# First expert products with weights stationary: two weight matrices fetched per tile from DRAM

## The chip, the core and the metric

The kernel runs on one NeuronCore of a Trainium2 chip. Its engines work side by side: PE (TensorE, matrix products), ACT (ScalarE), DVE (VectorE), POOL (GpSimd) and SP (SyncE, which here only issues DMAs). The metric is the device time of one execution in microseconds; of several runs the median is taken.

## The reference, cut to what matters

The input is 2048 tokens of 256 numbers (4 batches of 512). A mixture-of-experts block, an attention block and the same expert block again are added to it. All is float32.

```python
x = x + 0.5 * _L0_ffn_ref(_layernorm(x, axis=-1), gate, w0, w1, wo)
x = x + _L0_attn_ref(_layernorm(x, axis=-1), wq_a, q_a_norm_w, wq_b, wkv_a, kv_a_norm_w, wkv_b, wo_attn)
x = x + 0.5 * _L0_ffn_ref(_layernorm(x, axis=-1), gate, w0, w1, wo)

def _L0_ffn_ref(x, gate_kernel, w0_kernel, w1_kernel, wo_kernel):   # 8 experts, 256 -> 512 -> 256
    gate_logits = jnp.einsum('bsd,de->bse', x, gate_kernel)
    top_k_weights, top_k_indices = jax.lax.top_k(gate_logits, 2)
    top_k_weights = jax.nn.softmax(top_k_weights, axis=-1)
    combine = ...                      # the two weights at the two experts' places, else 0
    h0 = jnp.einsum('bsd,edm->bsem', x, w0_kernel)
    h1 = jnp.einsum('bsd,edm->bsem', x, w1_kernel)
    inter = jax.nn.silu(h0) * h1
    return jnp.einsum('bse,bsem,emd->bsd', combine, inter, wo_kernel)
```

## The kernel before, in words

Only the two chosen experts of a token are computed. The kernel sorts the (token, expert) pairs into tiles: up to 128 tokens that share one expert. Each of the two expert phases has 39 tiles (`NTILES`). A list of tiles (`list_tiles`) holds per tile the token rows (`idx`), the tokens' weights (`w`) and the offset `off` of the expert's columns in the stored weights, as an integer that an engine reads into a register. Each phase has two lists, made at different times, because the first tiles start before all tokens are routed.

The weights of all experts lie in SBUF for the whole kernel: `w_sb[0]`, `w_sb[1]` and `w_sb[2]` (w0, w1, wo), 4 MB each. `load_expert_weights` (L127) fetches them at the start on SP's queue, in loads of 1 MB.

`ffn_tiles` (L907) is a generator with one tile `j` per round:

- `gather(j + 2)` (L916): an indirect DMA of POOL fetches the token rows of the tile two rounds ahead.
- `hidden(j)` (L938): PE reads `off` (L940) and makes h0 and h1 (L951), with the turned tokens `xT` stationary (a weight of 128x128) and 512 weight columns moving, in two halves of the 256 inputs. The result has tokens as its 128 partitions. ACT takes the silu (L961), DVE the product `it` (L963).
- `turn(j + 1)` (L928): PE transposes the next tile's rows (L933), DVE copies them (L936).
- `project(j - 1)` (L974): four products with `wo` (L978) give `py`. They need the hidden numbers on the partitions, so `turn_hidden` (L966) had transposed `it` on PE (L969) and copied it on ACT (L971). DVE scales by the tokens' weights (L987) and POOL adds the rows into a DRAM tensor `acc_d` by an indirect DMA (L992); the last tiles of the second phase add into the output itself.
- `turn_hidden(it)` of tile j.

After each of the four parts the generator yields, and other work is put in there: in the first phase the routing of the later tokens and the first steps of attention, in the second the routing of the last batch (`beside.step`). Each engine executes its instructions in the order in which this program emits them; there is no scheduler after that. The same holds for SP, whose queue carries all plain loads and stores: the start's loads, a copy of x into `acc_d[0]` (L1283), the attention weights (`load_attention`), the reload of x from `acc_d[0]` (L109), the read of the routing table (L495), the stores of x into `acc_d[1]` (L1255), and the four copies of `acc_d[1]` to the output (L1004), issued when tile `final - 1` of the second phase has been projected.

A matrix product in float32 appears in the profile as two PE records, each with a weight load (PEld) of its own; a transposition as one.

Of the kernel before, what the change touches and what calls it, by code (L numbers as in the profile page):

```python
# [9 lines left out]
F32 = mybir.dt.float32  # L10
I32 = mybir.dt.int32
AF = mybir.ActivationFunctionType
# [4 lines left out]
P = 128  # L17
# [15 lines left out]
def kernel(  # L33
# [29 lines left out]
    WE = DC * MLP  # L63
# [6 lines left out]
    NTILES = (2 * NTOK + (P - 1) * NE) // P  # L70
# [15 lines left out]
    pp = ctx.enter_context(tc.tile_pool(name="p", bufs=2 * NT + LEAD))  # L86
# [3 lines left out]
    ps_a = ctx.enter_context(tc.tile_pool(name="ps_a", bufs=3, space=PSUM))  # L90
    ps_t = ctx.enter_context(tc.tile_pool(name="ps_t", bufs=2, space=PSUM))
# [30 lines left out]
    nc.scalar.dma_start(gate_sb[:, :, :NE], gate_k.rearrange("(c p) e -> p c e", p=P))  # L122


    w_sb = [wpool.tile([P, NE * WE], F32, name=f"w{i}_sb") for i in range(3)]

    def load_expert_weights(i):  # L127
        rows_of = (w0_k, w1_k, wo_k)[i].rearrange("e k m -> (e k) m")
        width = rows_of.shape[1]
        n = P * (2 * WE // width)  # L130
        for r in range(0, rows_of.shape[0], n):
            c0 = r // P * width
            nc.sync.dma_start(
                w_sb[i][:, c0 : c0 + 2 * WE].rearrange("p (k m) -> p k m", m=width),
                rows_of[r : r + n, :].rearrange("(k p) m -> p k m", p=P),
            )


    ident = const.tile([P, P], F32, name="ident")
# [510 lines left out]
    def put(pt, oh, first, last):  # L650
# [6 lines left out]
        )  # L657

    def route_first(ph, loads):


# [137 lines left out]
    def list_tiles(ph, n, m, split=0, read=None):  # L799
# [9 lines left out]
        last = m == B  # L809
        res = {"rows": NTOK + P if last else m * S}  # L810
# [4 lines left out]
        def parts():  # L815
# [91 lines left out]
    def ffn_tiles(f, jobs, final=None):  # L907

        n = len(jobs)
        xg, xT = {}, {}

        def gather(j):  # L916
            if j >= n:
                return
            res, i = jobs[j]
            xg[j] = ptp.tile([P, D], F32, tag="pt", name="xg")  # L920
            nc.gpsimd.indirect_dma_start(  # L921
                out=xg[j],
                out_offset=None,
                in_=xn_d[f][: res["rows"], :],
                in_offset=bass.IndirectOffsetOnAxis(ap=res["idx"][:, i : i + 1], axis=0),
            )

        def turn(j):  # L928
            if j >= n:
                return  # L930
            pt = ps_t.tile([P, DC, P], F32, tag="t", name="pt_x")
            for c in range(DC):
                nc.tensor.transpose(pt[:, c, :], xg[j][:, c * P : (c + 1) * P], ident)  # L933
            del xg[j]
            xT[j] = ptp.tile([P, DC, P], F32, tag="pt", name="xT")
            nc.vector.tensor_copy(xT[j], pt)  # L936

        def hidden(j):  # L938
            res, i = jobs[j]
            off = nc.values_load(  # L940
                res["off"][:, i : i + 1],
                engines=(mybir.EngineType.PE,),
                min_val=0,
                max_val=(NE - 1) * WE,
                skip_runtime_bounds_check_because="the offset of one of NE experts, or 0",
            )
            ph = []
            for w in range(2):
                p = ps_a.tile([P, MLP], F32, tag="a", name=f"h{w}")
                for c in range(DC):  # L950
                    nc.tensor.matmul(  # L951
                        p,
                        lhsT=xT[j][:, c, :],
                        rhs=w_sb[w][:, bass.ds(off + c * MLP, MLP)],
                        start=(c == 0),
                        stop=(c == DC - 1),
                    )
                ph.append(p)
            del xT[j]
            g = pp.tile([P, MLP], F32, tag="p", name="g")  # L960
            nc.scalar.activation(g, ph[0], AF.Silu)  # L961
            it = pp.tile([P, MLP], F32, tag="p", name="it")
            nc.vector.tensor_mul(it, g, ph[1])  # L963
            return off, it

        def turn_hidden(it):  # L966
            pt = ps_t.tile([P, MC, P], F32, tag="t", name="pt_i")
            for m in range(MC):
                nc.tensor.transpose(pt[:, m, :], it[:, m * P : (m + 1) * P], ident)  # L969
# [4 lines left out]
        def project(j, off, iT):  # L974
            res, i = jobs[j]
            py = ps_p.tile([P, D], F32, tag="p", name="py")
            for m in range(MC):
                nc.tensor.matmul(  # L978
                    py,
                    lhsT=iT[:, m, :],  # L980
                    rhs=w_sb[2][:, bass.ds(off + m * D, D)],
                    start=(m == 0),
                    stop=(m == MC - 1),
                )
            direct = final is not None and j >= final
            y = ptp.tile([P, D], F32, tag="pt", name="yo")
            nc.vector.tensor_scalar_mul(y, py, res["w"][:, i : i + 1])  # L987
            dst = flat_out if direct else acc_d[f][: res["rows"], :]
            held.append((dst, res["idx"][:, i : i + 1], y))
            if not direct or j >= final + HELD:  # L990
                for dst, idx, y in held:
                    nc.gpsimd.indirect_dma_start(  # L992
                        out=dst,
                        out_offset=bass.IndirectOffsetOnAxis(ap=idx, axis=0),
                        in_=y,
                        in_offset=None,
                        compute_op=ALU.add,
                    )
                held.clear()
            if final is not None and j == final - 1:  # L1000

                for r in range(0, NTOK, NTOK // 4):
                    r = slice(r, r + NTOK // 4)
                    nc.sync.dma_start(  # L1004
                        flat_out[r, :].rearrange("(p r) d -> p (r d)", p=P),
                        acc_d[f][r, :].rearrange("(p r) d -> p (r d)", p=P),
                    )

        held = []
        gather(0)  # L1010
        gather(1)
        yield -1
        turn(0)
        yield -1
        todo = None
        for j in range(n):
            gather(j + 2)
            off, it = hidden(j)
# [250 lines left out]

    list_a = route_first(one, loads)  # L1270

# [2 lines left out]
    jobs = [(list_a, i) for i in range(n_a)]  # L1274
# [46 lines left out]
    jobs = [(list_a, i) for i in range(n_a)]  # L1321
# [7 lines left out]
    for i, (b, h) in enumerate(items):  # L1329
# [13 lines left out]
        for kc in range(NT):  # L1343
# [3 lines left out]
            k = (i + 1) * NT + LEAD + kc  # L1347
# [114 lines left out]
```

## Time and profile before

| | |
|---|---|
| median of 3 runs | 1198.45 us (1195.29 to 1198.54) |
| the profiled execution's own time | 1194.49 us |
| its span | 1192.3 us |
| PE, DVE, ACT, POOL busy | 1115.8, 612.7, 452.3, 577.7 us |
| first products of the tiles (L951) | 624 records, 283.0 us |
| transpositions of the hidden numbers (L969) | 312 records, 47.9 us |
| products with wo (L978) | 624 records, 147.8 us |

The span is the time from the first to the last instruction of the profiled execution. In the rows of slices each digit is the busy share, in tenths, of one fortieth of the span. In the timeline a row gives start and duration in microseconds, the engine, the line of the kernel, the operation, what it writes and reads, and in brackets how long the engine had been idle before it and what ended that wait. PE rows of one line are merged; the duration of a merged row includes the tail of the last record, which overlaps with the next row.

### The profile page before, as it was taken

The numbers are of one execution on the slowest core, as the hardware profiler recorded it, in microseconds if no ns is written. First come the engines' busy times: TensorE is split into PE (matmuls) and PEld (weight loads), VectorE is DVE, ScalarE is ACT, GpSimd is POOL, SyncE is SP. The second block draws the span as 40 slices with busy tenths as digits, with TensorE's granted clock in tenths as the row PEclk, the third lists the DMA queues.
The fourth block names the chain that finished last, engine by engine and source line by source line (L and its number), as shares of the span: only waits on it lengthen the run. The fifth ranks groups of instructions, "written<-read, shape, count | busy, mean of one in ns | idle before, by whom it ended". The sixth has DMA issues, their size and how long they took to land. (4 is left out here: it accounts for less than half of the span.)

```text
span 1192.3 us, 15062 instructions
## 1 busy us (share of the span) xinstructions
PE 1115.8 (94%) x4704; PEld 631.8 (53%) x4704; DVE 612.7 (51%) x1673; ACT 452.3 (38%) x992; POOL 577.7 (48%) x645
## 2 busy tenths in 40 slices
PE   4889999999899999999999989899999899999995
PEld 3555666566445455444445545454455456666563
DVE  6463222344567666686666676657756343222221
ACT  4421221122554555554454544455454231121111
POOL 4244444355545454543566444475474246444342
PEclk8999999999999999998999989999999999999998
DMA  9943222322100000100000100001000124222422
GB/s 319 384 100 41 45 45 45 80 36 40 14 1 1 1 1 1 54 1 1 1 1 19 36 1 1 1 1 36 1 1 6 36 54 50 45 45 45 111 49 27
DMA packets 42141, 52.80 MB, mean 44 GB/s; under 512 B 10736, under 2 KB 34416, under 8 KB 41968
## 3 DMA queue, kind: packets, MB, share of 16 engines
q0 software_dynamic: 17184, 23.39, 11.8%
q1 hardware_dynamic: 24608, 28.45, 7.4%
q8 instruction: 40, 0.66, 0.2%
q14 instruction: 37, 0.30, 0.1%
q10 hardware_dynamic: 272, 0.01, 0.0%
HBM read 34.48 MB, written 21.54 MB: 47 GB/s over the span
## 5 line engine op out<-in xcount | busy, mean ns | idle before, releaser
L1160 POOL TENSOR_SCALAR pr<-pr,sm 128x512 f32<-128x512 f32 x256 | 177.8, 697 | 287.4 <-DVE sm L1159 242.3
L1155 ACT ACTIVATE pr<-ps,nm 128x512 f32<-128x512 f32 x256 | 176.5, 690 | 307.4 <-DVE nm L1152 281.2
L951 PE MATMUL h<-w_sb,xT 128*128 x624 | 283.0, 596 | 1.7 <-DVE xT L936 1.7
L1144 PE MATMUL ps<-k,q 128*128 128x512 f32 x512 | 274.9, 620 | 4.5 <-ACT pr L1155 4.5
L1152 DVE TENSOR_REDUCE nm<-ps 128x1 f32<-128x512 f32 x256 | 174.8, 683 | 102.6 <-PE ps L1144 101.4
L1166 PEld LDWEIGHTS pt<-ident,pr 128*128 128x128 f32 x1024 | 127.7, 142 | 157.4 <-issue 100.0
L992 POOL DMA_INDIRECT acc_d<-yo,idx x64 | 102.1, 1595 | 192.2 <-DVE yo L987 137.2
L963 DVE TENSOR_TENSOR it<-g,h 128x512 f32<-128x512 f32 x78 | 53.6, 687 | 248.0 <-PE h L951 237.5
L951 PEld LDWEIGHTS h<-w_sb,xT 128*128 128x128 f32 x624 | 113.3, 192 | 116.0 <-issue 112.7
L1166 PE MATMUL pt<-ident,pr 128*128 128x128 f32 x1024 | 156.6, 276 | 16.1 <-ACT pT L1173 13.9
L978 PE MATMUL py<-w_sb,iT 128*128 x624 | 147.8, 380 | 3.0 <-ACT iT L971 3.0
L971 ACT COPY iT<-pt_i 128x512 f32<-128x512 f32 x78 | 45.8, 587 | 269.3 <-PE pt_i L969 254.7
L1179 PE MATMUL po<-pT,low 128*64 128x512 f32 x512 | 123.8, 605 | 0.0
L978 PEld LDWEIGHTS py<-w_sb,iT 128*128 128x128 f32 x624 | 112.6, 190 | 17.1 <-ACT iT L971 4.1
L1144 PEld LDWEIGHTS ps<-k,q 128*128 128x128 f32 x512 | 80.2, 192 | 77.3 <-ACT pr L1155 36.9
L1159 DVE RECIPROCAL sm<-sm 128x1 f32<-128x1 f32 x256 | 41.3, 161 | 102.4 <-ACT pr L1155 101.9
L921 POOL DMA_INDIRECT xg<-xn_d,idx x78 | 77.8, 997 | 31.0 <-issue 18.8
L1171 DVE COPY pT<-pt 128x512 f32<-128x512 f32 x128 | 87.1, 680 | 2.2 <-PE pt L1166 2.2
L961 ACT ACTIVATE g<-h 128x512 f32<-128x512 f32 x78 | 46.6, 597 | 88.9 <-PE h L951 86.6
L1173 ACT COPY pT<-pt 128x512 f32<-128x512 f32 x128 | 73.9, 577 | 2.3 <-PE pt L1166 2.3
L987 DVE TENSOR_SCALAR yo<-py,wt 128x256 f32<-128x256 f32 x78 | 37.6, 482 | 57.9 <-PE py L978 57.9
L1193 PE MATMUL pwo<-wvo,oT 128*128 128x256 f32 x256 | 65.4, 398 | 1.8 <-ACT oT L1241 1.7
(220 smaller groups left out, 1122.0 us busy)
## 6 DMA issues: line engine op xcount, KB each, us to landing
w_sb<-in_L_ffn_w_kernel_dram SPq DMA_DIRECT2D x8, 1024.0 KB, 12.6
w_sb<-in_L_ffn_wo_kernel_dram SPq DMA_DIRECT2D x4, 1024.0 KB
x<-_attn_hidden_states_dram SPq DMA_DIRECT2D x4, 512.0 KB
xn_d<-xn POOLq DMA_DIRECT2D x8, 256.0 KB
x<-acc_d SPq DMA_DIRECT2D x4, 512.0 KB
acc_d<-x SPq DMA_DIRECT2D x4, 512.0 KB
xn_d<-xn SPq DMA_DIRECT2D x8, 256.0 KB, 3.7
out_dram<-acc_d SPq DMA_DIRECT2D x4, 512.0 KB, 7.3
```

The costliest lines, as they stand in the source:

```text
L921: nc.gpsimd.indirect_dma_start(out=xg[j], out_offset=None, in_=xn_d[f][: res["rows"], :], in_offset=bass.IndirectOffsetOnAxis(ap=res["idx" ...
L951: nc.tensor.matmul(p, lhsT=xT[j][:, c, :], rhs=w_sb[w][:, bass.ds(off + c * MLP, MLP)], start=(c == 0), stop=(c == DC - 1),)
L978: nc.tensor.matmul(py, lhsT=iT[:, m, :], rhs=w_sb[2][:, bass.ds(off + m * D, D)], start=(m == 0), stop=(m == MC - 1),)
L992: nc.gpsimd.indirect_dma_start(out=dst, out_offset=bass.IndirectOffsetOnAxis(ap=idx, axis=0), in_=y, in_offset=None, compute_op=ALU.add,)
L1144: nc.tensor.matmul(ps, lhsT=qT[:, t * P : (t + 1) * P], rhs=st[b]["k"][h % 2], start=True, stop=True,)
L1152: nc.vector.tensor_reduce(nm, ps, AX.X, ALU.max, negate=True)
L1155: nc.scalar.activation(pr, ps, AF.Exp, bias=nm, accum_out=sm)
L1160: nc.gpsimd.tensor_scalar(pr, pr, sm, 1.0, ALU.mult, ALU.mult)
L1166: nc.tensor.transpose(pt[:, t * P : (t + 1) * P], probs[t][:, kc * P : (kc + 1) * P], ident)
L1171: nc.vector.tensor_copy(s, pt)
L1173: nc.scalar.copy(s, pt)
L1179: nc.tensor.matmul(po[j * RANK : (j + 1) * RANK], lhsT=st[b]["low"][:, kc, 1, :], rhs=pts[j], start=(kc == 0), stop=(kc == NT - 1),)
```

## The change

w0 and w1 no longer lie in SBUF. `gather` reads the tile's first row `row` (256 times the expert's number, made by DVE for each list from the same product as `off`) into a register of SP, and loads this expert's w0 and w1, 512 KB each, from DRAM into one of three buffers. `hidden` makes h0 and h1 with 128x128 pieces of these weights stationary and the 128 tokens moving, so that the hidden numbers come out on the partitions; `turn_hidden` is dropped. `off` is read by PE in `project`, and `wo` alone is loaded at the start.

```diff
+    ws = ctx.enter_context(tc.tile_pool(name="ws", bufs=3))
...
-    w_sb = [wpool.tile([P, NE * WE], F32, name=f"w{i}_sb") for i in range(3)]
-
-    def load_expert_weights(i):
...
+    wo_sb = wpool.tile([P, NE * WE], F32, name="wo_sb")
+
+    def load_expert_outputs():
...
+            res["row"] = rt.tile([1, NTILES], I32, tag=f"row{last}", name="row")
+            nc.vector.tensor_scalar_mul(res["row"][:, :n], px[:1, 2, :n], D / WE)
...
         def gather(j):
             if j >= n:
                 return
             res, i = jobs[j]
+            row = nc.values_load(
+                res["row"][:, i : i + 1],
+                engines=(mybir.EngineType.SP,),
...
+            )
+            w01[j] = ws.tile([P, 2, DC, MLP], F32, tag="ws", name="w01")
+            for w, src in enumerate((w0_k, w1_k)):
+                nc.sync.dma_start(
+                    w01[j][:, w],
+                    src.rearrange("e k m -> (e k) m")[bass.ds(row, D), :].rearrange(
+                        "(c p) m -> p c m", p=P
+                    ),
+                )
...
         def hidden(j):
+
+            ph = []
+            for w in range(2):
+                p = ps_a.tile([P, MC, P], F32, tag="a", name=f"h{w}")
+                for m in range(MC):
+                    for c in range(DC):
+                        nc.tensor.matmul(
+                            p[:, m, :],
+                            lhsT=w01[j][:, w, c, m * P : (m + 1) * P],
+                            rhs=xT[j][:, c, :],
+                            start=(c == 0),
+                            stop=(c == DC - 1),
+                        )
+                ph.append(p)
+            del xT[j], w01[j]
+            g = pp.tile([P, MC, P], F32, tag="p", name="g")
+            nc.scalar.activation(g, ph[0], AF.Silu)
+            it = pp.tile([P, MC, P], F32, tag="p", name="it")
+            nc.vector.tensor_mul(it, g, ph[1])
+            return it
+
+        def project(j, it):
             res, i = jobs[j]
             off = nc.values_load(
...
-            ph = []
-            for w in range(2):
-                p = ps_a.tile([P, MLP], F32, tag="a", name=f"h{w}")
-                for c in range(DC):
-                    nc.tensor.matmul(
-                        p,
-                        lhsT=xT[j][:, c, :],
-                        rhs=w_sb[w][:, bass.ds(off + c * MLP, MLP)],
...
-        def turn_hidden(it):
-            pt = ps_t.tile([P, MC, P], F32, tag="t", name="pt_i")
-            for m in range(MC):
-                nc.tensor.transpose(pt[:, m, :], it[:, m * P : (m + 1) * P], ident)
-            iT = pp.tile([P, MC, P], F32, tag="p", name="iT")
-            nc.scalar.copy(iT, pt)
-            return iT
...
                 nc.tensor.matmul(
                     py,
-                    lhsT=iT[:, m, :],
-                    rhs=w_sb[2][:, bass.ds(off + m * D, D)],
+                    lhsT=it[:, m, :],
+                    rhs=wo_sb[:, bass.ds(off + m * D, D)],
...
-            todo = (j, off, turn_hidden(it))
+            todo = (j, it)
...
     folded = load_folded()
-    load_expert_weights(0)
...
-        for i in (1, 2):
-            load_expert_weights(i)
+        load_expert_outputs()
```

More of the change, by code (lines that the diff above doesn't have):

```diff
@@ L122 @@
     nc.scalar.dma_start(gate_sb[:, :, :NE], gate_k.rearrange("(c p) e -> p c e", p=P))
-    w_sb = [wpool.tile([P, NE * WE], F32, name=f"w{i}_sb") for i in range(3)]
-    def load_expert_weights(i):
-        rows_of = (w0_k, w1_k, wo_k)[i].rearrange("e k m -> (e k) m")
-        width = rows_of.shape[1]
-        n = P * (2 * WE // width)
+    wo_sb = wpool.tile([P, NE * WE], F32, name="wo_sb")
+    def load_expert_outputs():
+        rows_of = wo_k.rearrange("e k m -> (e k) m")
+        n = P * (2 * WE // D)
         for r in range(0, rows_of.shape[0], n):
-            c0 = r // P * width
+            c0 = r // P * D
             nc.sync.dma_start(
-                w_sb[i][:, c0 : c0 + 2 * WE].rearrange("p (k m) -> p k m", m=width),
+                wo_sb[:, c0 : c0 + 2 * WE].rearrange("p (k m) -> p k m", m=D),
                 rows_of[r : r + n, :].rearrange("(k p) m -> p k m", p=P),
@@ L913, in ffn_tiles @@
         n = len(jobs)
-        xg, xT = {}, {}
+        xg, xT, w01 = {}, {}, {}
         def gather(j):
@@ L919, in gather @@
             res, i = jobs[j]
+            row = nc.values_load(
+                res["row"][:, i : i + 1],
+                engines=(mybir.EngineType.SP,),
+                min_val=0,
+                max_val=(NE - 1) * D,
+                skip_runtime_bounds_check_because="the first row of one of NE experts, or 0",
+            )
[7 more added lines that the diff above has]
+                )
             xg[j] = ptp.tile([P, D], F32, tag="pt", name="xg")
@@ L946, in hidden @@
             )
-            ph = []
-            for w in range(2):
-                p = ps_a.tile([P, MLP], F32, tag="a", name=f"h{w}")
-                for c in range(DC):
-                    nc.tensor.matmul(
-                        p,
-                        lhsT=xT[j][:, c, :],
-                        rhs=w_sb[w][:, bass.ds(off + c * MLP, MLP)],
[L955 to L964, printed above, removed]
-        def turn_hidden(it):
-            pt = ps_t.tile([P, MC, P], F32, tag="t", name="pt_i")
-            for m in range(MC):
-                nc.tensor.transpose(pt[:, m, :], it[:, m * P : (m + 1) * P], ident)
-            iT = pp.tile([P, MC, P], F32, tag="p", name="iT")
-            nc.scalar.copy(iT, pt)
-            return iT
-        def project(j, off, iT):
-            res, i = jobs[j]
             py = ps_p.tile([P, D], F32, tag="p", name="py")
@@ L1017, in ffn_tiles @@
             gather(j + 2)
-            off, it = hidden(j)
+            it = hidden(j)
             yield j
```

## The prediction

> **What bounds the kernel now.** I read the page's head first, then the expert stages in order of time, then the shapes on the PE, then the queues. All numbers come from the profiled execution: span 1192.3 us, time 1194.49 us, which is 0.3% under the median of the runs shown (1198.45). The sum below is made against the span; the 2.2 us around it stay.
>
> ```profile
> span 1192.3 us, 15062 instructions
> PE 1115.8 (94%) x4704; PEld 631.8 (53%) x4704; DVE 612.7 (51%) x1673; ACT 452.3 (38%) x992; POOL 577.7 (48%) x645
> PE   4889999999899999999999989899999899999995
> DMA  9943222322100000100000100001000124222422
> ```
>
> The PE is near full everywhere but in the first slices; DMA is full only in the first two. The two expert stages (about 46 to 303 us and 943 to 1181 us) hold 78 tiles: L951 has 624 records, 8 to a tile. The table by stretches shows the PE busy 90.0 of 90 us between 120 and 210, and 85.0 of 85 between 1020 and 1105, so there a tile costs what its PE work costs. From 46 to 110 us it is busy 55.3 of 64.
>
> One tile in the timeline (start, duration, engine, line):
>
> ```profile
> 152.01 0.38 PE L933 MATMUL pt_x<-ident,xg 128*128 128x128 f32 x2
> 152.23 1.89 PE L978 MATMUL py<-w_sb,iT 128*128 x8
> 153.96 0.60 PE L969 MATMUL pt_i<-ident,it 128*128 128x128 f32 x4
> 154.40 3.60 PE L951 MATMUL h<-w_sb,xT 128*128 x8
> ```
>
> Read starts, not durations, since the pipeline's tail overlaps. The next pt_x starts at 157.84. So h takes 3.44 us (0.430 a record of 512 columns), pt_x 0.22, py 1.73, pt_i 0.44: 5.83 us a tile, with no gap.
>
> The shape that the change asks for, 128 columns against a freshly loaded 128x128 f32 weight, is already in the program, at L1074:
>
> ```profile
> 257.08 1.95 PE L1074 MATMUL pj<-wqc,xnT 128*128 128x128 f32 x16
> 258.87 0.60 PE L969 MATMUL pt_i<-ident,it 128*128 128x128 f32 x4
> ```
>
> Sixteen records take 258.87 - 257.08 = 1.79 us: 0.112 each. A quarter of a 512-column record would be 0.1075, so the extra weight loads nearly hide.
>
> **The change part by part.**
>
> *Products.* Per tile 8 records of 0.430 (3.44 us) become 32 of 0.112 (3.58 us): +0.14 us. Bounds for one record: 0.1075 (a quarter of L951's) and 0.117 (L1074's load busy time, 7.5 us over 64, if loads pace a longer stream). They give 0.00 and +0.30. I take 0.112, the same shape at full clock. A rule speaks against the change: the Trainium skill, page "TensorE: Matmul & The Clock Gate", section "Back-to-back issue gap", puts a sustained stream at about 81 ns for 128 columns and 131 ns for 512. Four narrow ones would then cost 2.5 times a wide one, h would take 8.5 us, and 78 tiles would lose about 395 us. Here the ratio is 4 x 0.112/0.430 = 1.04, in f32 and in this program, so the sum uses the trace.
>
> *Transposition.* Four L969 records go: -0.44 us of PE per tile. The ACT copy iT (L971, 587 ns) goes too, off the path since ACT is under half busy. Two exceptions. At the hand-over to attention the last py (309.53) waits 2.31 us for that copy; I count 1.5 us of it, since the scores behind it have waits of their own. At the very end I count no extra gain: the last scatter follows the one before by 4.44 us (1178.68 to 1183.12), its landing, however early py comes.
>
> *Registers.* On the PE four of eight register operations a tile go (42 to 51 ns, L951) and the register load (L940, 301 ns) moves behind the products. No gap shows at either place now, 3.4 us of matmuls being queued; 0. On DVE one small row product per list comes in (L900's like takes 0.15 us), four times; the first stands ahead of the first loads, 0.15 us.
>
> Over 78 tiles: (0.14 - 0.44) x 78 = -23.4 us. Where the PE waits anyway (46 to 110 us, some ten tiles, and the second stage's first few) I give back 2.0.
>
> *DMA.* Per tile SP issues one register load and two loads of 512 KB. Three buffers let tile j+3 start when the products of j end, about 13 us before they are needed. Price of one MB:
>
> ```profile
> DMA packets 7918, 13.28 MB, mean 379 GB/s; under 512 B 512, under 2 KB 3340, under 8 KB 7916
> ...
> q1 hardware_dynamic: 7261, 11.29, 91.2%
> ```
>
> This is the stretch from 10 to 45 us: 1.05 MB at 379 GB/s is 2.8 us, half of a 5.5 us tile. Gather and scatter use 27% now (120 to 210 us), so about 0.77 in all. The skill's page "DMA: Bandwidth & Descriptors", section "Measured (HBM→SBUF, 128 partitions, SWDGE, issued from GpSimd)", gives 6.15 us for 1 MB and advises batches of at least that size. At 6.15 us per tile the queue would be the bound, +0.33 us over today's 5.82, some +25 us. The loads here run two tiles ahead back to back on SP's queue, so the trace's rate counts and the latency is covered; 0 in the steady part.
>
> *SP's order.* Loads now stand in line with SP's other work, and three places cost.
>
> First start. The row is known when off is, at 39.5 us. Two tiles' loads (2 MB) are issued then; the queue is free, since 8 MB of early loads are gone (today SP issues expert weights until 48). They land about 45 to 47; h starts at 46.6 today. About 0. But tile 2's load stands behind the 2 MB copy into acc_d and all attention loads, which take SP from 51.6 to 66.2 us today. Starting near 44, SP is free near 59, and tile 2's weights land near 63.5. Its products start at 62.28 today and about a microsecond earlier without pt_i: +2 (bounds 0 and 4).
>
> The reload of x from acc_d near 211 us waits for a scatter, and tile loads are queued behind it. They have over two tiles to spare. It also shares the queue, and POOL's next scatter waits for it; today this already costs one PE wait of 1.09 us at 228.93. +1 (0 to 2).
>
> The copies to the output:
>
> ```profile
> 1101.63 1.59 POOL L992 DMA_INDIRECT acc_d<-yo,idx  x1 [2.93 <-DVE yo L987]
> 1105.25 2.45 SPq L1004 DMA_DIRECT2D out_dram<-acc_d  x4
> 1112.74 3.60 PE L951 MATMUL h<-w_sb,xT 128*128 x8
> 1115.54 1.62 POOL L992 DMA_INDIRECT out_dram<-yo,idx  x1 [8.50 <-DMA out_dram<-acc_d]
> ```
>
> SP waits for the scatter, issues four copies until 1107.7, and only then loads the weights of the tile whose products are shown at 1112.74. Those bytes follow 2 MB of copies in the same queue (traffic ends at 1113), so the first half lands near 1116. The new timetable wants it near 1111.7. PE stall 4 us. In return today's PE wait of 1.42 us at 1129.40, for a gather behind the backlog of scatters, should vanish. +2.6 (0 to 6).
>
> **Sum.** -23.4 - 1.5 + 2.0 + 0.15 + 2 + 1 + 2.6 = -17 us. Span about 1175, its time about 1177; carried to the median (+4), 1181 us.
>
> **The rivals.**
>
> *The gain in full:* SP's three places stay covered. -23.4 - 1.5 + 2 = -23, about 1175 by the median; 1170 if a record costs 0.110. For it: each place has only a few microseconds' shortfall. Against: the copies' place is short by arithmetic.
>
> *Loads pace the long stream at 0.117:* +0.30 - 0.44 = -0.14 a tile, -11 us, given back by SP's places and the early tiles: about 1194, near no change. For it: 32 loads in a row are longer than any in this trace. Against: L1074's load starts are 0.11 apart all through.
>
> *Slower: the scatter chain on POOL becomes the bound.* Each scatter into acc_d waits for the landing of the one before. Where there is a backlog the rows stand at their minimum:
>
> ```profile
> 1124.65 1.57 POOL L992 DMA_INDIRECT out_dram<-yo,idx  x1 [2.99 <-DVE yo L987]
> 1129.11 1.58 POOL L992 DMA_INDIRECT out_dram<-yo,idx  x1 [1.57 <-DVE it L963]
> 1133.54 1.57 POOL L992 DMA_INDIRECT out_dram<-yo,idx  x1 [1.53 <-DMA out_dram<-yo,idx]
> ```
>
> 4.45 us apart, with almost no other traffic. Behind them on POOL stands the next gather, and for it the PE. A saturated queue stretches such transfers: the first gather took from 39.63 to 45.60, a late one from 1126.52 to 1129.40, so up to +3.1 us. The chain decides from 5.53 us on, and the kernel gets slower when stretching exceeds about 1.4 us. At +1.6 us (half of the bound) the tile is 6.05, +0.23 x 78 = 18 us over today, minus the hand-over's gain and plus SP's places about 1220. Against it: weights move from about 1.5 us after h ends for 2.8 us, while the scatter's bytes start about 2.4 us into the next h; by these times they overlap some half microsecond, so the chain would be near 5 us.
>
> That the change doesn't do what it says is not a case here: the instruction order has 16 products of 128x128 to a tile, each issued as two records, and no L969.
>
> **How the numbers follow.** Forecast (about -17) 0.55; gain in full 0.12; loads pace 0.13, split 0.04 faster, 0.06 the same, 0.03 slower; scatter chain 0.20, of which 0.02 only eats the gain up. About 0.3% is what a measurement of this kernel tells from no change. Faster 0.71, same 0.08, slower 0.21. The range runs from the full gain with the cheapest record, 1170, to the lower half of the scatter case, 1207; the forecast's own range is 1174 to 1188.
>
> **What would show it.** Right: between 120 and 210 us and 1020 to 1105 the PE stays full; starts of h are 5.5 us apart, 3.6 us from h to pt_x; pt_i is gone; one PE wait for a weight load after the copies, of about 4 us, and a small one at tile 2. Wrong: h over 3.8 us (loads), waits of pt_x for xg tile after tile with scatters over 5.5 us apart (chain), or waits for weight loads in the steady part (DMA).

## The result, and the profile after

The kernel got slower: 1213.24 us by the median of 4 runs (1209.25 to 1215.49) against 1196.87 us of the kernel before (4 runs beside it), a ratio of 1.0136 with a 95% interval of 1.0100 to 1.0172. The forecast was 1181 us. The profiled execution of after took 1213.32 us, its span 1211.3, which is 19.0 us over the span before; its mean granted clock was 0.969 (before 0.982).

The head of the page, and of its slices of the span the PE, its clock and the DMA:

```profile
span 1211.3 us, 18471 instructions
PE 1107.8 (91%) x6264; PEld 775.0 (64%) x6264; DVE 612.3 (51%) x1677; ACT 406.0 (34%) x914; POOL 577.5 (48%) x645
...
PE   4888999799999999999899989999999997999795
...
PEclk8989999899999999998999989999999998999898
DMA  9776888665100000100000100000002587887762
```

The PE is busy for 8 us less than before, and yet the span is longer. In both expert stages the digits of the DMA row, mostly 2 and 3 before, are now 5 to 8, and the PE row has three 7s where it had none.

One tile in the timeline (columns as in the timeline of before; L963 is now the first products, L951 pt_x, L989 py):

```profile
151.77 3.73 PE L963 MATMUL h<-xT,w 128*128 128x128 f32 x32
155.34 0.38 PE L951 MATMUL pt_x<-ident,xg 128*128 128x128 f32 x2
155.56 1.89 PE L989 MATMUL py<-wo_sb,it 128*128 x8
157.29 0.94 PE L963 MATMUL h<-xT,w 128*128 128x128 f32 x7
```

From h to pt_x it is 3.57 us for 32 records, 0.112 each; from one h to the next 5.52 us. The forecast tile was 5.83 - 0.30 = 5.53 us. What else the stretches show is in the table by stretches (busy time of PE, PEld, DVE, ACT and POOL with their instructions, granted clock, DMA share, GB/s):

```profile
120.00:210.00 90.00, 90.00 (x690) 86.70 (x689) 24.08 (x48) 10.15 (x17) 42.68 (x34) 1.00 0.87 241
210.00:303.00 93.00, 84.26 (x600) 76.06 (x599) 35.62 (x93) 12.13 (x21) 42.18 (x34) 0.96 0.65 185
...
1105.00:1181.00 76.00, 67.99 (x489) 63.53 (x488) 17.41 (x34) 7.07 (x12) 28.39 (x22) 0.96 0.72 228
```

The last two of these stretches before:

```profile
210.00:303.00 93.00, 91.86 (x357) 56.20 (x356) 37.63 (x96) 20.87 (x36) 46.29 (x37) 1.00 0.27 50
...
1105.00:1181.00 76.00, 73.89 (x282) 46.04 (x280) 19.12 (x38) 14.81 (x25) 30.32 (x23) 1.00 0.33 68
```

Between 120 and 210 us nothing is lost although the DMA engines are 0.87 busy. In the two stretches that have other traffic of their own the PE is idle for 8.7 and 8.0 us (before, 1.1 and 2.1), and its clock is lower.

The start of each tile's first products, set against before, gives the ledger. In an even stretch it falls by 0.305 us a tile; every jump above that is a loss. The fourth column is the same jump in the first experiment below (the products alone), in which no tile loads weights:

| place | forecast | loss measured | of it without loads | who waits in after |
|---|---|---|---|---|
| tile 2 | +2 | +3.5 | 0.4 | PE 2.47 us at 62.02, for its weights |
| tiles 5 to 8, a list of tiles is read | part of the 2.0 given back | +5.2 | 3.5 | PE 0.97 at 103.46 for xg, 3.90 at 106.92 for the list |
| tile 28, after the reload of x | +1 | +7.1 | 2.0 | PE 6.07 at 227.31 for xg |
| tile 33 | none | +2.3 | 0.2 | PE 2.12 at 270.20 for xT |
| tiles 47 to 51, routing of the last batch | none | +11.3 | 0.0 | PE 1.73, 3.47 and 2.71 from 995 to 1020 |
| tile 67, after the copies to the output | +2.6 with the next row | +5.5 | 0.0 | PE 5.32 at 1122.20, for its weights |
| tiles 68 to 77 | in the row above | +7.2 | 3.9 | PE five short waits for xg |
| hand-over to attention | -1.5 | -1.5 | -2.6 | |

The seven losses sum to 42 us, against a gain of 0.305 x 78 = 24; 10 of the 42 come without any load. The rest up to the 19.0 us of the span are the hand-over, the first tiles of the second stage, where the PE waits anyway and nothing is won (1.5), and small differences at other tiles. For the wait at tile 2 the profile names an operation of DVE (L373) that is no input of the products. Their xT was ready at 61.42, and SP issued their weights only at 58.93, so it is read here as a wait for the weights; in the variant below that asks for them a tile earlier it is gone.

The PE's waits, by what it waited for (total, times, longest):

```profile
PE pt_x L951 <- DMA xg<-xn_d,idx: 12.4, 8, 6.1
...
PE h L963 <- DMA w<-in_L_ffn_w_kernel_dram: 5.3, 1, 5.3
```

Before, pt_x's waits for gathers were 3.3 us in all. And POOL's waits, with two rows that before did not have among its longest ten:

```profile
POOL acc_d L1003 <- DMA acc_d<-yo,idx: 18.4, 5, 5.2
POOL out_dram L1003 <- DMA out_dram<-yo,idx: 15.4, 5, 4.4
```

These are scatters that wait for the landing of the scatter before, and behind each stands the next gather. The copies to the output, the place shown of before, read now:

```profile
1115.71 2.46 SPq L1015 DMA_DIRECT2D out_dram<-acc_d  x4
1118.76 26.61 SPq L932 DMA_DIRECT2D w<-in_L_ffn_w_kernel_dram  x12
1127.52 5.84 PE L963 MATMUL h<-xT,w 128*128 128x128 f32 x32 [5.32 <-DMA w<-in_L_ffn_w_kernel_dram]
```

The weights issued at 1118.76 behind the copies' 2 MB are there at 1127.5. Then the products run at a lower clock: 5.68 us to the next pt_x at 1133.20 instead of 3.57. The granted clock stands at 0.50 in five such stretches of the two stages in which it was 1.00 before, each behind one of the waits (3.90, 6.07, 1.73, 2.71 and 5.32 us). It does not follow every wait: after the one of 3.47 us it stayed at 1.00. Of a table of the five, the last row and the sum:

```profile
1127.50:1131.70 4.20, 4.18 (x19) 4.20 (x20) 0.00 (x0) 0.39 (x1) 0.38 (x1) 0.50 1.07 385
sum 18.20, PE 18.17 PEld 16.34 DVE 3.37 ACT 0.39 POOL 3.39; mean PE 3.63 PEld 3.27 DVE 0.67 ACT 0.08 POOL 0.68
```

The 19 records of that row take 0.22 us each, twice the 0.112 of the even stretch. So by an estimate half of the 18.2 us, some 9 of the 42, is the lower clock; the rest is mostly the waits themselves. The scatters behind the copies:

```profile
1126.26 1.62 POOL L1003 DMA_INDIRECT out_dram<-yo,idx  x1 [8.88 <-DMA out_dram<-acc_d]
1133.98 1.59 POOL L1003 DMA_INDIRECT out_dram<-yo,idx  x1 [6.11 <-issue]
1139.80 1.57 POOL L1003 DMA_INDIRECT out_dram<-yo,idx  x1 [4.23 <-DVE it L975]
...
1145.20 1.58 POOL L1003 DMA_INDIRECT out_dram<-yo,idx  x1 [2.52 <-DVE it L975]
```

They follow each other after 7.7, 5.8 and 5.4 us. Before, the backlog at this place had 4.45 us from one to the next, and so caught up with the tiles; now it does not.

### The profile page after: what moved, and what is told of

Read it like the earlier page. It is cut to its first block, busy times and chain, and to the rows that moved or that the text cites. A ratio compares the mean times of both kernels' runs of the same rounds, so it can differ in the third digit from the quotient of the medians.

```text
span 1211.3 us, 18471 instructions
## 1 busy us (share of the span) xinstructions
PE 1107.8 (91%) x6264; PEld 775.0 (64%) x6264; DVE 612.3 (51%) x1677; ACT 406.0 (34%) x914; POOL 577.5 (48%) x645
## 5 line engine op out<-in xcount | busy, mean ns | idle before, releaser
L963 PE MATMUL h<-xT,w 128*128 128x128 f32 x2496 | 300.9, 280 | 14.1 <-DVE xT L954 5.7
L963 PEld LDWEIGHTS h<-xT,w 128*128 128x128 f32 x2496 | 297.7, 197 | 21.6 <-DVE xT L954 8.0
L1155 PE MATMUL ps<-k,q 128*128 128x512 f32 x512 | 271.9, 614 | 4.5 <-ACT pr L1166 4.5
L989 PE MATMUL py<-wo_sb,it 128*128 x624 | 152.7, 389 | 0.8 <-PE pt_x L951 0.2
L989 PEld LDWEIGHTS py<-wo_sb,it 128*128 128x128 f32 x624 | 115.1, 194 | 17.9 <-issue 4.4
L1190 PEld LDWEIGHTS po<-pT,low 128*64 128x64 f32 x512 | 31.6, 138 | 49.0 <-issue 49.0
```

Source lines behind the costliest of these rows:

```text
L963: nc.tensor.matmul(p[:, m, :], lhsT=w01[j][:, w, c, m * P : (m + 1) * P], rhs=xT[j][:, c, :], start=(c == 0), stop=(c == DC - 1),)
L989: nc.tensor.matmul(py, lhsT=it[:, m, :], rhs=wo_sb[:, bass.ds(off + m * D, D)], start=(m == 0), stop=(m == MC - 1),)
L1155: nc.tensor.matmul(ps, lhsT=qT[:, t * P : (t + 1) * P], rhs=st[b]["k"][h % 2], start=True, stop=True,)
L1190: nc.tensor.matmul(po[j * RANK : (j + 1) * RANK], lhsT=st[b]["low"][:, kc, 1, :], rhs=pts[j], start=(kc == 0), stop=(kc == NT - 1),)
```

## The experiments

Ratios are to the kernel before, run beside each group of kernels on one chip (its medians there were 1194.42, 1197.31 and 1200.73 us). Three theories stood at the start. *Traffic:* 1 MB a tile on the shared DMA engines delays what POOL's gathers and scatters move. *Order:* the loads stand in SP's line behind other work and come late. *Products:* narrow products cost more than the even stretch shows.

### Which half of the change costs

**The products alone.** The kernel before with the new products: all weights at the start, as before, no transposition; each tile uses expert 0's w0 and w1. The products, set against those of the change:

```diff
-                        lhsT=w01[j][:, w, c, m * P : (m + 1) * P],
+                        lhsT=w_sb[w][:, c * MLP + m * P : c * MLP + (m + 1) * P],
```

> The kernel before with the new products and without the transposition; all weights are loaded at the start as before the change, and every tile uses the first expert's (values not the reference's). Unlike the run without loads (1194 us, whose first tile's gather waited for a copy into acc_d that SP now issued 10 us earlier), SP's start is that of before. Theory: the products do save 0.3 us a tile and the start took it back there: 1180 to 1186, h of the first tile at about 46 us. If it is near 1194 again, the saving is lost somewhere else and not by the start.

Measured: 1184.31 us (4 runs), ratio 0.9887 (0.9832 to 0.9941). So the products and the dropped transposition are worth 13 us by themselves. In its profile 0.305 us a tile are won through both stages, and some is given back with no load in sight. The PE waits 4.8 us for the list at tile 7 (before 1.7), 2.2 us for a gather after the reload of x (before 1.09), and 3.5 us for a gather behind the backlog of scatters after the copies (before 1.42):

```profile
107.85 0.38 PE L876 MATMUL px<-sel,tab 128*128 128x30 f32 x2 [4.78 <-DVE tab L510]
226.49 0.44 PE L933 MATMUL pt_x<-ident,xg 128*128 128x128 f32 x2 [2.22 <-DMA xg<-xn_d,idx]
1118.32 0.53 PE L933 MATMUL pt_x<-ident,xg 128*128 128x128 f32 x2 [3.54 <-DMA xg<-xn_d,idx]
```

Faster tiles only come to these places earlier. The whole 24 us were not to be had.

**The loads alone.** The change's loads under the products of before, with moving weights and the transposition:

```diff
+                        lhsT=xT[j][:, c, :],
+                        rhs=w01[j][:, w, c, :],
...
+            todo = (j, turn_hidden(it))
```

> The other half of the change alone: products with tokens stationary and the transposition as before the change, but w0 and w1 fetched per tile as in the change. If the loads are the loss, they cost here about what they cost in the changed kernel, some 43 us less what a longer tile (5.82 instead of 5.52 us) leaves as slack: 1225 to 1240 us. If the narrow products are the loss, it stays near 1197.

Measured: 1227.06 us (4 runs), 1.0257 (1.0189 to 1.0326), 31 us slower. The two halves add up: -1.1% and +2.6% make +1.5%, and the change has +1.4%. *Products* is out. The profile is of an execution of 1218.35 us, below this median. In it the jumps lie at the same places (tile 28 +4.0, tiles 47 to 50 +9.6, 67 to 77 +8.0), and between them a tile starts exactly 5.82 us after the other: 3.02 us behind before at tiles 7 to 27, 16.06 at tiles 50 to 66.

**Half the bytes.** w0 of expert 0 stays in SBUF for all tiles, w1 is loaded per tile.

```diff
-            for w, src in enumerate((w0_k, w1_k)):
+            for w, src in enumerate((w1_k,)):
...
-                            lhsT=w01[j][:, w, c, m * P : (m + 1) * P],
+                            lhsT=(w01[j][:, 0] if w else w0_sb)[:, c, m * P : (m + 1) * P],
```

> The changed kernel with half the bytes: w0 of the first expert is loaded once and used for all tiles (values not the reference's), w1 is fetched per tile, with the same register load and the same waits on SP. Theory traffic (the weights' bytes stretch POOL's gathers and scatters on the shared DMA engines): waits of PE for xg fall to well under half, scatters in a backlog stand about 5 us apart instead of 6, total 1180 to 1190. Theory order (the loads stand too late in SP's queue): the order is the same, so the PE waits for weights at tile 2 (2.5 us) and after the output copies (5.3 us) stay to within a microsecond or two.

Measured: 1191.16 us (20 runs), 0.9967 (0.9945 to 0.9990). Beside the products alone (0.9887) half the bytes cost 0.8%, all of them 2.5%; and yet a load of each tile stands in SP's line as in the change. The wait for weights after the copies is still 3.9 us.

**No loads per tile; expert 0's weights loaded once at the start,** and none of the others.

```diff
+    def load_first_expert():
+        for w, src in enumerate((w0_k, w1_k)):
+            nc.sync.dma_start(w01_sb[:, w], src[0].rearrange("(c p) m -> p c m", p=P))
...
-                            lhsT=w01[j][:, w, c, m * P : (m + 1) * P],
+                            lhsT=w01_sb[:, w, c, m * P : (m + 1) * P],
```

> The changed kernel without the loads per tile: w0 and w1 of the first expert are loaded once and used for all tiles, so the values are not the reference's; products, order and everything else as changed. If the loss comes with the loads (their bytes on the DMA engines, or their place in SP's queue), it vanishes here and the PE's own saving stays: about 1197 - 24 = 1173 us, starts of h 5.5 us apart in the even stretches, no PE wait over 1.5 us for xg. If narrow products themselves are the cost, it stays near 1213.

Measured: 1194.08 us (20 runs), 0.9989 (0.9964 to 1.0014), far from what was expected. The reason is mostly at the start. Before, SP is held by the loads of all experts' weights and issues the 2 MB copy of x into acc_d at 51.55. Freed of them it issues it at 41.53, beside the first gathers: pt_x waits 4.79 us for xg, the first products start 5.9 us late and run at a lower clock (h 6.5 us), and at tile 1 it is 8.1. The products alone, above, keep the start's loads and do not show this. So this kernel does not measure what it was meant to. But it shows a start that is 8 us later when 2 MB move beside the first gathers.

### Order or traffic

**Weights three tiles ahead, in four buffers.** The loads of tile 2 are out ahead of the acc_d copy, and each load has a tile more of time. Gathers are two ahead, as in the change.

```diff
-    ws = ctx.enter_context(tc.tile_pool(name="ws", bufs=3))
+    ws = ctx.enter_context(tc.tile_pool(name="ws", bufs=4))
...
-            gather(j + 2)
+            ahead("w", j + 3, fetch)
+            ahead("x", j + 2, gather)
```

> The changed kernel with four weight buffers instead of three and the weights asked for three tiles ahead, gathers still two. Theory order: both PE waits for weights vanish and with them about 9 us: 1204 or less. Theory traffic: the waits for weights vanish too, but the waits of pt_x for xg (12.4 us in all) and the backlog of scatters stay or grow, since the same bytes move: 1203 to 1212.

Measured: 1223.78 us (4 runs), 1.0192 (1.0109 to 1.0275). That is no better than the change (the intervals overlap), though the wait at tile 2 is gone and the one after the copies smaller (1.61 us). The profile is of an execution of 1227.92 us, above the median, and in it the even stretch breaks:

```profile
120.00:210.00 90.00, 82.64 (x603) 76.19 (x602) 22.49 (x44) 8.45 (x15) 34.83 (x29) 1.00 0.72 222
```

7.4 us of PE are lost there, with fewer bytes a microsecond than in the change. The timelines of POOL and SP, first of this kernel, then of after, show what differs:

```profile
177.39 0.95 SPq L937 DMA_DIRECT2D w<-in_L_ffn_w_kernel_dram  x2
177.40 1.58 POOL L1011 DMA_INDIRECT acc_d<-yo,idx  x1 [2.78 <-DMA acc_d<-yo,idx]
...
183.12 0.94 SPq L937 DMA_DIRECT2D w<-in_L_ffn_w_kernel_dram  x2
...
185.34 1.59 POOL L1011 DMA_INDIRECT acc_d<-yo,idx  x1 [5.06 <-DMA acc_d<-yo,idx]
...
189.79 1.58 POOL L1011 DMA_INDIRECT acc_d<-yo,idx  x1 [1.57 <-DMA acc_d<-yo,idx]
```

```profile
177.61 0.95 SPq L932 DMA_DIRECT2D w<-in_L_ffn_w_kernel_dram  x2
...
180.32 1.58 POOL L1003 DMA_INDIRECT acc_d<-yo,idx  x1 [2.63 <-DVE yo L998]
...
183.12 0.94 SPq L932 DMA_DIRECT2D w<-in_L_ffn_w_kernel_dram  x2
...
185.84 1.59 POOL L1003 DMA_INDIRECT acc_d<-yo,idx  x1 [2.63 <-DVE yo L998]
```

A scatter issued with the loads (177.40 and 177.39) holds the next one until 185.34, 7.94 us later. One issued 2.2 us after loads (185.34 after 183.12) is followed after 4.45 us. In after, the scatters of the even stretch come 2.7 us after the loads, and wait for nothing but their own rows. The change runs in step there: the loads start when the products end and free a buffer, and the scatter comes when py is done. By the code this step hangs on the three buffers, and on a POOL that isn't late. That the PE loses time where the step is lost is shown only without slack: the last variant under "Can slack take it up" also loads three tiles ahead, and its even stretch stays full.

**Loads issued by ACT.** The loads and the register load leave SP's line; all else is the change.

```diff
-                engines=(mybir.EngineType.SP,),
+                engines=(mybir.EngineType.Activation,),
...
-                nc.sync.dma_start(
+                nc.scalar.dma_start(
```

> The changed kernel with the tile's register load and its two weight loads issued by ACT instead of SP: same bytes, same time of asking, but no longer in line with SP's copies and attention loads. Theory order: tile 2's wait and the wait after the output copies go, 1204 or less. Theory traffic: those two shrink, but the copies and the weights now share the engines at one time and the gathers and scatters are stretched as before: 1207 to 1218.

Measured: 1226.39 us (4 runs), 1.0226 (1.0170 to 1.0282). Part of it is this kernel's own: ACT waits for the first row, and with it its copies of `wvo` (9.53 us), so the first products start 6.7 us late. But the jump at tile 28 is +6.6 us, nearly as in the change (+7.1), though the loads no longer stand behind the reload of x there. And what the PE waits for is gathers (pt_x for xg, 29.1 us in 11 waits), not weights (1.8 us). Only after the copies to the output does the issuer matter: the jump of 5.5 us at tile 67 is gone here, and 6.7 us come back at tile 70. *Order* explains the waits at tiles 2 and 67, 9 us of the 42 at most.

### Where the loads cost

**Loads only in the even stretches, and their complement.** Two kernels: a tile loads its weights, or it uses one copy of expert 0's.

```diff
+    def loaded(f, j):
+        even = 9 <= j < 27 if f == 0 else 13 <= j < 28
+        return (f == 0 and j < 2) or even
...
+            if loaded(f, j):
...
+            else:
+                w01[j] = w01_sb
```

The second has `or not even`.

> The change, but a tile loads its weights only where the trace of after showed an even stretch: tiles 9 to 26 (the first stage, about 110 to 215 us), 52 to 66 (the second, about 1023 to 1105 us), and the first two; 35 loads of 78. All other tiles use one copy of expert 0's w0 and w1, so their values are not the reference's. If a load beside an even tile costs nothing, and the whole loss arises where the order of POOL's scatters against the loads is disturbed: 9 to 13 us faster than before, as with all weights fixed (ratio 0.989 to 0.993), and no wait of the PE between 120 and 210 us. If every load costs the same (the 29 us between fixed weights and the change, over 78 tiles): 35 x 0.37 = 13 us given back, so even with before (ratio 0.998 to 1.003).

> The complement: the tiles that used the fixed copy load their weights, and tiles 9 to 26 and 52 to 66 use the copy of expert 0 (their values are not the reference's); the first two load as in the change; 45 loads of 78. If the loss arises only in the disturbed places: all of it is here, 13 to 17 us slower than before (ratio 1.011 to 1.014), with the waits at tiles 2, 5 to 8, 28, 47 to 50, 67 to 77 as in after. If every load costs the same: 45 x 0.37 = 17 us given back of 13, about 4 us slower (ratio 1.002 to 1.005).

Measured: 35 loads in the even stretches, 1192.86 us (11 runs), 0.9955 (0.9929 to 0.9981); the other 45, 1219.17 us (4 runs), 1.0170 (1.0121 to 1.0219). The complement has all of the change's loss: to spare 33 loads of 78 in the even stretches brings nothing (1.0170 beside 1.0136, the intervals overlap). The first kernel is 5 us faster than before by its ratio and lies between the two expectations. Beside the products alone (0.9887) it loses 0.7%, 8 us. Its even stretches are not quite free: three waits of pt_x of 0.3 to 1.1 us stand in them (89.07 of 90 busy between 120 and 210, 83.77 of 85 after 1020), and their jumps sum to 3.9 us. So the loads of the disturbed places are the greater part of the loss. Those of the even places cost little, and in the change itself, whose jumps there are 0.1 us in each stage, nothing.

What happens at such a place, at tile 28 of after, by the stretch from 221 to 234 us:

```profile
221.00:234.00 13.00, 6.93 (x52) 6.29 (x50) 2.77 (x7) 0.60 (x1) 3.80 (x3) 0.87 0.90 302
```

The same stretch before, and POOL at that place:

```profile
221.00:234.00 13.00, 11.91 (x46) 7.20 (x45) 5.21 (x15) 2.37 (x4) 6.04 (x5) 1.00 0.36 77
...
224.03 1.59 POOL L992 DMA_INDIRECT acc_d<-yo,idx  x1 [5.37 <-DMA x<-acc_d]
225.93 0.99 POOL L921 DMA_INDIRECT xg<-xn_d,idx  x1 [0.30 <-issue]
228.68 1.58 POOL L992 DMA_INDIRECT acc_d<-yo,idx  x1 [1.76 <-DVE it L963]
```

At the reload of x POOL's scatter waits 5.4 us before and 5.5 in after. Before, the scatters held up then clear at 4.4 to 4.7 us each. In after, three tiles' loads come between 221.3 and 227.9, two of them held behind the reload in SP's line, and a gather that took 3.0 us (225.93 to pt_x at 228.93) takes 6.6 (226.79 to 233.37); the next scatter comes 7.9 us after the one before:

```profile
221.34 6.93 SPq L932 DMA_DIRECT2D w<-in_L_ffn_w_kernel_dram  x6
...
224.89 1.59 POOL L1003 DMA_INDIRECT acc_d<-yo,idx  x1 [5.53 <-DVE yo L998]
226.79 0.99 POOL L939 DMA_INDIRECT xg<-xn_d,idx  x1 [0.30 <-issue]
232.79 1.58 POOL L1003 DMA_INDIRECT acc_d<-yo,idx  x1 [5.01 <-DMA acc_d<-yo,idx]
...
233.37 0.69 PE L951 MATMUL pt_x<-ident,xg 128*128 128x128 f32 x2 [6.07 <-DMA xg<-xn_d,idx]
```

### Can slack take it up

**Gathers three ahead,** weights as in the change:

```diff
-            gather(j + 2)
+            ahead("w", j + 2, fetch)
+            ahead("x", j + 3, gather)
```

> The changed kernel with gathers asked for three tiles ahead instead of two; weights two ahead in three buffers as in the change. If the loss reaches the PE by late gathers (pt_x waits for xg: 12.4 us, and the slow clock after each), these waits go and it gains 10 to 15 us: 1198 to 1204. If the chain of scatters is the bound at those places, gathers asked for earlier only stand behind the same scatters: within 4 us of 1213.

Measured: 1211.07 us (4 runs), 1.0104 (1.0050 to 1.0158); its interval overlaps that of the change. The waits of pt_x for xg are gone, those of h for weights at tile 2 (2.57 us) and after the copies (6.10) are not. And h waits for xT (15.2 us in all), because the copy of xT needs a buffer that a row not yet scattered holds:

```profile
235.43 0.42 DVE L962 COPY xT<-pt_x 128x256 f32<-128x256 f32 x1 [5.08 <-DMA acc_d<-yo,idx]
```

**Gathers four ahead, and pools of six buffers each for xg and yo;** then the same with weights three ahead.

```diff
+    xgp = ctx.enter_context(tc.tile_pool(name="xg", bufs=6))
+    yop = ctx.enter_context(tc.tile_pool(name="yo", bufs=6))
...
+            ahead("x", j + 4, gather)
```

> The change with slack around POOL: gathers four tiles ahead, and pools of their own, six buffers each, for the gathered rows xg and for the rows yo to be scattered (in the change they share eight buffers with xT, so that a late scatter holds back the copy of the next tile's xT). Weights are loaded two tiles ahead as in the change. If the loss is the scatter chain's being late at some places, and it is under 5.5 us on the mean, slack of four tiles takes it up: pt_x's waits for xg (15.9 us in after) and h's waits for xT (5.7) go, and the waits for weights at tile 2 and after the copies stay (about 8 us): 1190 to 1200, even with before or up to 5 us faster. If the shared DMA engines have no spare time for what the loads push aside, the chain stays late and the waits come back at the end of each stage: 1207 to 1213, as with gathers three ahead.

> The same slack, and the weights loaded three tiles ahead into four buffers. If the slack takes up what the chain is late, the earlier loads do no harm here and take the waits at tile 2 and after the copies too: 1183 to 1193, faster than before by 5 to 13 us. If loads that are out of step with the scatters lengthen the chain beyond the tile (5.5 us) in the even stretch, as the spacings of 7.9 and 4.4 us in the variant with four buffers suggest (6.2 on the mean), the slack only delays it: after some six tiles POOL is behind again, and the time is that of that variant, 1210 to 1224.

Measured: 1213.64 us (4 runs), 1.0135 (1.0079 to 1.0190), and 1218.44 us (4 runs), 1.0165 (1.0116 to 1.0215). Neither is faster than the change. In the first, tile 28 passes without a jump: the slack does what it should. But POOL is no less late, and POOL has other work, in order, that has no slack. Its part of the rotation of k (L1064 to L1068) stands behind the late scatters and gathers; ACT needs it for the next step of attention, and the silu is queued behind that on ACT:

```profile
272.68 0.60 ACT L1105 ACTIVATE sq<-pj 128x512 f32<-128x512 f32 x1 [18.18 <-POOL k L1068]
```

The PE then waits 10.82 us at 264.85. In the second stage the table of the routing, scattered by the same POOL, comes late in the same way (pn_c at L822 waits 12.7 us). The waits are as large as in the change, and in fewer places. The wait at tile 33 of the change is the first of these on a smaller scale: there ACT waits 9.47 us for k.

The second, with weights three tiles ahead, has no wait for weights at all, no jump at tile 28, and full even stretches:

```profile
120.00:210.00 90.00, 90.00 (x689) 86.69 (x688) 24.57 (x49) 9.56 (x16) 40.78 (x32) 1.00 0.85 251
```

Between 153.10 and 185.84 its scatters come 5.46 us apart on the mean, against 6.24 (152.36 to 189.79) in the variant with four buffers and no slack. So the chain did not fall behind again after some six tiles, as one of the two expectations had it. The loss is nearly all at work in which POOL has a part besides the tiles: the PE waits 7.65 us for the list at tile 7, 15.71 us behind the rotation of k, and 12.20 us for the table of the routing.

### Fewer bytes with the right values

w0 of all experts stays in SBUF and ACT copies the expert's part for each tile (1.05 us); w1 is loaded as in the change.

```diff
+            nc.scalar.copy(w0c[j], w0_sb[:, bass.ds(at, WE)])
...
-            for w, src in enumerate((w0_k, w1_k)):
+            for w, src in enumerate((w1_k,)):
```

> Reference values, half the bytes: w0 stays in SBUF and ACT copies the tile's expert (1024 columns a partition) into one of two buffers by a register's offset; w1 is fetched per tile as in the change. If bytes are what costs, it lands where the half-bytes run did (1191), give or take 4; the ACT copy, about 1.1 us a tile on an engine that is idle for over 4 us of it, should not show. If ACT's copies come late, h waits for ACT tile after tile and it is over 1200.

Measured: 1206.53 us (20 runs), 1.0072 (1.0049 to 1.0095): some 9 us slower than before, and half as much over it as the change. The loads halved take the waits down, as the half with fixed weights did; its start is 3.3 us late (tile 0). ACT's copy stands in the line of the silu; what that costs was not measured apart. No version with the reference's values was found that beats the kernel before.

## Why the prediction was wrong

The forecast was -17 us. Its part for products, transposition, hand-over and early tiles, -23.4 - 1.5 + 2.0 = -23, measured -13 (the products alone). Its part for the loads, +5.75, measured some +30 (from 0.9887 to 1.0136). So both terms for what is given back were too small, the second by more.

**Products and transposition: right.** +0.14 - 0.44 = -0.30 a tile was forecast, -0.305 measured, and 0.112 us a record. The rule of the Trainium skill's page "TensorE: Matmul & The Clock Gate" ("Back-to-back issue gap"), by which h would take 8.5 us, fails here: h takes 3.57. Loads do not pace the long stream at 0.117 either.

**The steady part at 0: right,** with the DMA at 0.87 busy instead of 0.77. The 6.15 us for 1 MB in the skill's page "DMA: Bandwidth & Descriptors" (section "Measured (HBM→SBUF, 128 partitions, SWDGE, issued from GpSimd)") do not bound it: a tile's 1 MB comes every 5.52 us, and the PE waits for nothing.

**Early tiles: "I give back 2.0" was too small.** It was asked only where the PE waits in the kernel before. In the products alone 10 us are given back: 3.5 at the list, 2.0 at tile 28 (and 1.1 at the next), 3.9 after the copies. The list there comes at 107.85, before at 107.03, so faster tiles only wait for it. With the loads it comes at 110.82: the last table scatter of POOL that it needs goes out at 99.67 instead of 96.67.

**"SP's order": the step that failed.** It took the places for matters of SP's line, and priced each by when the weights land: 2 + 1 + 2.6 = 5.6 us. For tile 2 and for tile 67 that is the right mechanism, with the sizes off: 3.5 instead of 2 at tile 2, and a wait of 5.32 instead of 4 at tile 67, with 2.1 us of slow clock after it. But the reload of x was sized at 1 us because the weights had "over two tiles to spare". They had; what came late was the gather, which took 6.6 us instead of 3.0 beside three tiles' loads (7.1 us lost, 2.0 of them without loads). And the wait of 1.42 us at the backlog of scatters, which "should vanish", became five waits; without any load it is one of 3.5. The routing of the last batch was not on the list at all: POOL scatters tables there, eight of them between 983 and 1006 us before, and with the loads beside them 11.3 us are lost, without loads none. The prediction asked of each place whether the weights are late, not who else has bytes under way there.

**The scatter chain: right as a mechanism, wrong in its form.** "Stretching up to +3.1 us" was the bound; 7.9 - 4.45 = 3.5 was measured where loads and scatter start together. It was costed as an evenly spread half of that on 78 tiles and argued away by the times of the even stretch, where loads and scatter miss each other. The argument was sound there and was used everywhere. Where POOL is late, a scatter falls among the next loads, and the backlog, which before cleared at 4.45 us in a tile of 5.82, clears at 5.4 us and more in a tile of 5.52. That one late scatter makes the next later is read from these spacings; no run shows it by itself.

**The hand-over, the rows, the registers: right.** -1.5 at the hand-over; no wait at the register loads.

What stays open: whether the loads hold up the gathers and scatters in the DMA engines, in their queues or at the memory. Half the bytes cost a third, which speaks for the bytes, but no run tells these apart. And whether the wish to keep the step could be met by an order written by hand, scatter first and loads after, was not tried.

## What to carry to other kernels

Here a transfer that fitted into the mean of the DMA engines was free only while it kept step with the transfers that others wait for, or while these had slack. So price such a transfer not at the even tile but at every place with traffic or work of its own (a reload, a copy, a table), and ask there for the gathers and scatters, not only for the new load. Price also what a faster stage gives back at things that come at their own time: here 10 of 24 us. And slack given to one consumer of an engine that works in order moved the wait to the next consumer.

## What was not expected of the hardware

- The PE's clock: after 5.32 us of PE idle the 32 records of h took 5.68 us instead of 3.57, with a granted clock of 0.50; over the whole execution the mean granted clock fell from 0.982 to 0.969.
- More time ahead made it worse where nothing else had slack: with loads one tile earlier the even stretch lost 7.4 us of 90, by a scatter whose successor came after 7.94 us instead of 4.45. With gathers four ahead the same loads lost nothing there.
- In f32, four records of 128 columns with a weight load each cost 1.04 of one of 512 columns (0.112 and 0.430 us), and the PE's load row was 96% busy (86.70 of 90) without becoming the bound.
